# Two transformer layers on one core: how layer 0 keeps the exponentials of its eight chosen entries

## The chip, the cores and the metric

The kernel runs on one core of a Trainium2 chip. The metric is the device time of one execution in microseconds (us): the median of three runs, and beside it one execution taken by the hardware profiler, from which every duration of a single instruction comes. All data are fp32.

## The reference, cut to what matters

Two transformer layers work on 4 sequences of 512 tokens of width 512. Each layer adds an attention and a mixture of experts to its input. The change lies in the attention of layer 0, which has 16 heads of width 128. Each query of a head attends to two things: the keys of its own and the previous 128 tokens (the local part), and, among 128 entries that each compress 4 tokens, the 8 with the largest scores (the sparse part):

```python
sc = jnp.einsum('bhsd,bcd->bhsc', q, ck) * scale
sc = jnp.where(causal, sc, NEG)
tv, ti = jax.lax.top_k(sc, TOPK)                      # TOPK = 8
sel = (tv > NEG / 2).astype(sc.dtype)
m = jnp.max(tv, axis=-1, keepdims=True)
e = jnp.exp(tv - m) * sel
pw = e / jnp.maximum(e.sum(axis=-1, keepdims=True), 1e-09)
v_g = cv[jnp.arange(Bq)[:, None, None, None], ti]
ctx_sparse = jnp.einsum('bhsk,bhskd->bhsd', pw, v_g)
...
merged = (ctx_sparse + ctx_local) * 0.5
out = merged.transpose(0, 2, 1, 3).reshape(Bq, Sq, NH * D) @ Wo + bo
```

The kernel doesn't gather the chosen entries. It keeps a row of exponentials over all entries that a query may see, in which those that are not chosen are zero, and multiplies that row by all entries' values. So what is needed of each row of scores s is exp(s) where s is among the eight largest, and zero elsewhere.

## The kernel before

**Stages.** The start loads tables and normalises tokens. Layer 0's attention then runs in 32 steps: 8 groups of two heads, and for each group the 4 sequences (the loop of lines 1101 to 1160). After that comes layer 1 (from line 1171). In the profile, step 0 begins near 59 us and step 31 ends near 1440 us, so a step takes some 43 us.

**A step.** In each step i the heads 0 and 1 of the step are attended, while the projections of step i + 1 are made in between (`project`, lines 650 to 745: products p into the PSUM tag "mm" of three banks, line 675; their sums u, qb and lv on VectorE, lines 710 to 742; root mean squares by ScalarE's squares, line 575, and GpSimd's power, lines 577 and 578; ScalarE's scaling, line 689; turning by TensorE, lines 695 and 701, and ScalarE's copies, lines 696 and 702). For each head:

- `scores` makes the scores of 128 queries by four tiles of entries: TensorE writes sp (line 758), VectorE adds the causal mask (line 761), which gives s, 128 x 320. The 320 columns are the visible entries of the four tiles, 32, 64, 96 and 128 of them (`SEEN`, line 45). The local scores st go through ScalarE's exponential (line 771) and GpSimd's 0/1 mask (line 775).
- Then for each of the four tiles VectorE finds the eight largest of each row (line 779) and writes a copy rep of s in which these eight are replaced by NEG = -1e30 (line 780).
- Line 782 compares s with rep: 1 where they are equal, that is where an entry wasn't chosen. Line 783 adds NEG times that to s. Line 784 (ScalarE) takes the exponential of s, 320 elements, which is zero where NEG was added.
- `turn` transposes the result (TensorE, line 793) and copies it to SBUF (ScalarE, lines 794 and 795). `context` multiplies it by the entries' values (line 814) and the local exponentials by the local values (lines 809 and 811), divides by the sums and adds the two (lines 818 to 827).

After both heads, `output7` multiplies by the output weights (line 873) and adds to acc on VectorE (line 884).

**What sets the order.** A scheduler of the framework orders each engine's instructions, and an engine takes them strictly in that order. A few instructions are pinned to the order of the program. Into the steps other work is laid by a list of places (`run0`): in steps 0 to 2 the layernorms and the compressed entries (`compress`, lines 590 to 640: wd on VectorE at line 608, wB on TensorE at line 611, ck at line 628), in steps 3 and 4 the routing (lines 299 to 454, long chains of small VectorE instructions), in steps 5 to 22 the experts of layer 0 (lines 513 to 540: products hp_r at line 529, their rescue from PSUM by VectorE at line 532), and after that the combining of experts' results and the layernorms and weights' sums of layer 1 (lines 1016 to 1032 and 1207 to 1208).

**Buffers.** The pool wk0 has two buffers of the tag "s" (one 128 x 320 row tile each) and one of the tag "rep". The small table nws (line 194), used only at the start, is laid into the buffer of "rep". Tags are of fixed size, the largest of their users.

Of the kernel before, what the change touches and what calls it, by code (L numbers as in the profile page):

```python
# [12 lines left out]
F32 = mybir.dt.float32  # L13
I32 = mybir.dt.int32
AF = mybir.ActivationFunctionType
ALU = mybir.AluOpType
# [4 lines left out]
P = 128  # L21
# [3 lines left out]
TC = S // P  # L25
# [12 lines left out]
NEG = -1e30  # L38

SEEN = [slice(96, 128), slice(128, 192), slice(0, 96), slice(192, 320)]  # L40
LIMIT = 60.0
SCALE0 = 1.0 / math.sqrt(D)
# [7 lines left out]
def two_layers(ctx: ExitStack, tc: tile.TileContext, a: dict, out: bass.AP, large: bass.AP):  # L50
# [4 lines left out]
    V, G, A, PE = nc.vector, nc.gpsimd, nc.scalar, nc.tensor  # L55
# [11 lines left out]
    wk0 = layer0.enter_context(tc.tile_pool(name="att0", bufs=2))  # L67
    setup = ExitStack()

    sp0 = setup.enter_context(tc.tile_pool(name="setup", bufs=2, side="right"))  # L70


    def psum(tag, name):
        return ps.tile([P, 512], F32, tag=tag, name=name, bufs={"mm": 3, "sc": 3, "tr": 2}[tag])
# [70 lines left out]
    R = D // 2  # L145
# [45 lines left out]
    t2c = sp0.tile([P, 1, R], F32, tag="t2c", name="t2c", bufs=1)  # L191


    nws = wk0.tile([P, 2, R], F32, tag="rep", name="nws", bufs=1)
    own_ = lambda w, n, lo, m: nws[:, w, ds(lo, m)].unsqueeze(1).to_broadcast([P, n, m])

    def scale_weights():
# [551 lines left out]
    def scores(i, h, qkT):  # L749

        g, b = steps[i]
        nm = f"{g}_{b}_{h}"
        sp = psum("sc", f"sp_{nm}")
        seen = SEEN
        for t in range(TC):
            PE.matmul(sp[:, seen[t]], lhsT=qkT[:, h, ts(t, P)], rhs=ckT[:, b, 0 : 32 * (t + 1)],  # L758
                      start=True, stop=True)
        s = wk0.tile([P, SEEN[TC - 1].stop], F32, tag="s", name=f"s_{nm}")  # L760
        V.tensor_tensor(s, sp[:, 0 : SEEN[TC - 1].stop], cmask, ALU.add)
        lT = wk0.tile([P, TC * 2 * P - P], F32, tag="lT", name=f"lT_{nm}")
        for half in range(2):
            st = psum("sc", f"st{half}_{nm}")
            for t in (2 * half, 2 * half + 1):
                n = 256 if t + 1 < TC else 128
                PE.matmul(st[:, ds((t % 2) * 256, n)], lhsT=qkT[:, HG + h, ts(t, P)],  # L767
                          rhs=qkT[:, h, ds(t * P, n)], start=True, stop=True)
            for c in range(2):
                n = 256 if half + c < 2 else 128  # L770
                A.activation(lT[:, ds(half * 512 + c * 256, n)], st[:, ds(c * 256, n)], AF.Exp,  # L771
                             scale=norm_k[(i, h)][2 * half + c])
            n = 384 if half else 512
            dst = lT[:, ds(half * 512, n)]
            G.tensor_tensor(dst, dst, lmask.rearrange("p a w j -> p (a w j)")[:, 0:n], ALU.mult)  # L775
        top = small.tile([P, TC, 8], F32, tag="top", name=f"top_{nm}", bufs=2)
        rep = wk0.tile([P, SEEN[TC - 1].stop], F32, tag="rep", name=f"rep_{nm}", bufs=1)
        for t in range(TC):
            V.max(top[:, t, :], s[:, seen[t]])
            V.match_replace(rep[:, seen[t]], top[:, t, :], s[:, seen[t]], NEG)  # L780

        V.tensor_tensor(rep, s, rep, ALU.is_equal)
        V.scalar_tensor_tensor(s, rep, NEG, s, ALU.mult, ALU.add)
        A.activation(s, s, AF.Exp, scale=SCALE0)
        return s, lT

    def turn(i, h, em):
# [313 lines left out]
    for i, (g, b) in enumerate(steps):  # L1101
# [8 lines left out]
        cT = qp.tile([P, HG, S], F32, tag="cT", name=f"cT_{g}_{b}", bufs=1)  # L1110
        nc.sync.dma_start(out=cv0s[i % 2][96:P, 0:D], in_=cv[0:32, b, 0:D])
        em0, lT0 = scores(i, 0, now)
        turn_last(1)
        if more:
# [4 lines left out]
            if b == 2 and g + 1 in groups:  # L1119
                groups[g + 1][0][0] = load_block(g + 1, "wA")  # L1120
        run0((i, 0))
        em1, lT1 = scores(i, 1, now)
        sT0 = turn(i, 0, em0)
        run0((i, 1))
# [1151 lines left out]
```

## Time and profile before

| what | value |
|---|---|
| median of 3 runs | 2059.24 us (2058.99 to 2063.63) |
| the profiled execution | 2060.04 us, its span 2058.2 us |
| clock granted to TensorE | 0.995 |
| VectorE's row operations at lines 782 and 783, 64 each | 64.3 us and 42.9 us |
| ScalarE's exponential of s, line 784, 64 | 30.1 us |

TensorE is the engine "PE" of the profile (weight loads "PEld"), VectorE is "DVE", ScalarE "ACT", GpSimd "POOL". A line of the groups reads: line, engine, operation, output <- inputs with shapes, count | busy us, mean ns of one | idle time of the engine just before these instructions, and what ended it. A line of the timeline reads: start in us, duration in us, engine, line, operation, and in brackets the idle time before it and the instruction that ended that. A line of the windows reads: from:to, length, and each engine's busy us with its number of instructions.

### The profile page before, as it was taken

The page shows a single profiled execution, that of the slowest core. Times are in us where ns is not written, and L with a number is a line of the kernel's source. Part 1 is how long each engine was busy: PE and PEld are TensorE (multiplying, and loading weights), DVE is VectorE, ACT ScalarE, POOL GpSimd, SP SyncE. Part 2 cuts the span into 40 slices and gives each one's busy share as a digit, 9 for nine tenths or more (in the row PEclk, how much of TensorE's full clock was granted, in tenths as well). Part 3 has the DMA queues.
Part 4 walks back from the last instruction along what each step waited for, and adds up shares of the span by engine and source line. Part 5 has one row for each costly group of instructions (what it writes and reads, how often), then busy time and mean ns, then how long its engine had stood idle before and what let it go on. Part 6 is the DMA issues. An engine that isn't in the chain of part 4 may idle for free.

```text
span 2058.2 us, 28987 instructions
## 1 busy us (share of the span) xinstructions
PE 1982.5 (96%) x9514; PEld 1276.0 (62%) x9514; DVE 1545.9 (75%) x3799; ACT 864.3 (42%) x2600; POOL 745.4 (36%) x761
## 2 busy tenths in 40 slices
PE   7999999999999999999999998999999999999998
PEld 4666667777777777776667776776434445445442
DVE  7889987777776777786678888887696555557675
ACT  4544444444444444444444444454143432433332
POOL 4332235443332333334343444244114432422550
PEclk9999999999999999999999999999999999999999
DMA  7112133332433343244543222121317775773451
GB/s 251 58 42 62 32 123 114 134 131 93 136 118 119 114 144 116 93 136 174 189 161 116 73 88 67 48 73 62 120 32 264 258 257 204 261 245 117 151 160 58
DMA packets 98911, 267.29 MB, mean 130 GB/s; under 512 B 14400, under 2 KB 27840, under 8 KB 87488
## 3 DMA queue, kind: packets, MB, share of 16 engines
q0 software_dynamic: 27072, 148.91, 21.6%
q1 hardware_dynamic: 70528, 114.34, 16.6%
q10 hardware_dynamic: 1152, 2.10, 0.3%
q8 instruction: 78, 1.28, 0.3%
q14 instruction: 81, 0.66, 0.1%
HBM read 222.05 MB, written 42.73 MB: 129 GB/s over the span
## 4 chain that ended last, share of the span: by engine, by line
PE 73%; DVE 12%; ACT 4%; POOL 3%; issue 2%; DMA 1%; ACTq 0%; DVEq 0%; SPq 0%; POOLq 0%
PE p L675 21%; PE hp_r L529 12%; PE st L767 4%; PE ox L873 3%; PE st L1316 2%; PE oz L873 2%; PE qp L1292 2%; PE sp L758 2%; PE cx L1330 2%; DVE pS L1336 2%; PE ca L811 2%; PE o L1399 1%; PE trm_r L517 1%; ACT sq L575 1%; PE vp L1252 1%
## 5 line engine op out<-in xcount | busy, mean ns | idle before, releaser
L529 PE MATMUL hp_r<-we_r,xT_r 128*128 128x512 f32 (+1 forms) x592 | 224.7, 596 | 3.0 <-ACT xT_r L519 2.5
L481 POOL DMA_INDIRECT xr_r<-xnd,rows_r x72 | 87.5, 1216 | 348.1 <-PE trm_r L517 305.7
L775 POOL TENSOR_TENSOR lT<-lT,lmask 128x512 f32<-128x512 f32 (+1 forms) x128 | 152.1, 1196 | 150.7 <-ACT lT L771 150.6
L675 PE MATMUL p<-wT,x 128*128 128x384 f32 x512 | 179.8, 494 | 1.1 <-DVE wT L119 1.1
L675 PE MATMUL p<-wB,x 128*128 128x384 f32 x512 | 176.3, 488 | 3.0 <-DVE u L731 3.0
L675 PE MATMUL p<-wA,xnT 128*128 128x384 f32 x512 | 174.0, 490 | 0.1
L575 ACT ACTIVATE sq<-qb 128x128 f32<-128x128 f32 x384 | 118.9, 310 | 109.2 <-DVE qb L711 54.5
L1318 ACT ACTIVATE pT<-st 128x1024 f32<-128x1024 f32 x128 | 123.2, 1013 | 62.5 <-PE st L1316 56.8
L529 PEld LDWEIGHTS hp_r<-we_r,xT_r 128*128 128x128 f32 (+1 forms) x592 | 83.2, 170 | 99.0 <-issue 92.3
L675 PEld LDWEIGHTS p<-wB,x 128*128 128x128 f32 x512 | 93.9, 191 | 67.0 <-issue 9.9
L675 PEld LDWEIGHTS p<-wT,x 128*128 128x128 f32 x512 | 94.9, 194 | 63.4 <-issue 6.8
L675 PEld LDWEIGHTS p<-wA,xnT 128*128 128x128 f32 x512 | 95.1, 192 | 59.8 <-issue 1.9
L689 ACT ACTIVATE qb<-qb,ss 128x128 f32<-128x128 f32 x256 | 81.9, 390 | 107.3 <-POOL ss L578 103.8
L519 ACT COPY xT_r<-trm_r 128x512 f32<-128x512 f32 x72 | 41.8, 580 | 194.7 <-PE hp_r L529 181.9
L767 PE MATMUL st<-qkT 128*128 128x256 f32 (+1 forms) x512 | 116.0, 354 | 1.3 <-ACT qkT L702 1.3
L771 ACT ACTIVATE lT<-st,ss 128x256 f32<-128x256 f32 (+1 forms) x128 | 49.3, 444 | 158.2 <-PE st L767 158.1
L545 POOL DMA_INDIRECT row_r<-yd,slot_r x64 | 74.7, 1168 | 83.1 <-DVE row_r L1433 38.8
L767 PEld LDWEIGHTS st<-qkT 128*128 128x128 f32 x512 | 92.5, 191 | 12.0 <-ACT qkT L702 1.6
L578 POOL TENSOR_TENSOR ss<-ss,nhalf 128x6 f32<-128x6 f32 x64 | 94.3, 1474 | 5.3
L577 POOL TENSOR_SCALAR ss<-ss 128x6 f32<-128x6 f32 x64 | 31.1, 486 | 163.1 <-ACT sq L575 162.7
L675 PE MATMUL p<-wT,xnT 128*128 128x384 f32 x256 | 88.0, 487 | 0.0
L884 DVE TENSOR_TENSOR acc<-acc,ox 128x512 f32<-128x512 f32 (+1 forms) x96 | 82.3, 857 | 5.0 <-PE ox L873 4.4
(381 smaller groups left out, 4737.6 us busy)
## 6 DMA issues: line engine op xcount, KB each, us to landing
x<-xsd SPq DMA_DIRECT2D x112, 256.0 KB, 3.0
yd<-yr_r SPq DMA_DIRECT2D x72, 256.0 KB, 4.7
wA<-in_wA SPq DMA_DIRECT2D x16, 384.0 KB, 3.7
wB<-in_wB SPq DMA_DIRECT2D x16, 384.0 KB, 7.3
xnd<-xn SPq DMA_DIRECT2D x24, 256.0 KB, 2.0
accd<-acc SPq DMA_DIRECT2D x18, 256.0 KB, 2.0
acc<-in_x SPq DMA_DIRECT2D x16, 256.0 KB, 5.5
Wo<-in_Wo SPq DMA_DIRECT2D x8, 512.0 KB, 3.7
```

The costliest lines, as they stand in the source:

```text
L481: G.indirect_dma_start(out=out, out_offset=None, in_=src, in_offset=at_rows(idx))
L529: PE.matmul(hp[ts(h, m), :], lhsT=xT[:, k, ts(h, m)], rhs=w[:, ts(k, HID)], start=(k == 0), stop=(k == KC - 1))
L545: G.indirect_dma_start(out=x, out_offset=None, in_=self.yd, in_offset=at_rows(self.r.slot[:, k, n : n + 1]))
L575: A.activation(sq, x[:, h, :], AF.Square, accum_out=ss[:, h : h + 1])
L578: pin(G.tensor_tensor(ss, ss, nhalf[:, 0:n], ALU.pow))
L675: PE.matmul(p, lhsT=x[:, k, ts(c, P)], rhs=w[:, k, :], start=(k == 0), stop=(k == 1))
L689: A.activation(x[:, j, :], x[:, j, :], AF.Copy, scale=sq[t][:, j : j + 1])
L767: PE.matmul(st[:, ds((t % 2) * 256, n)], lhsT=qkT[:, HG + h, ts(t, P)], rhs=qkT[:, h, ds(t * P, n)], start=True, stop=True)
L775: G.tensor_tensor(dst, dst, lmask.rearrange("p a w j -> p (a w j)")[:, 0:n], ALU.mult)
L873: PE.matmul(p[:, ts(c, 256)], lhsT=left[:, ts(c, P)], rhs=right, start=new and c == 0, stop=True, skip_group_check=True)
L884: V.tensor_tensor(own, own, p, op)
L1318: A.activation(pt[:, ts(pair, 2), :], st, AF.Exp, scale=SCALE1)
```

## The change

The chosen entries are no longer marked. s and rep become the halves of one tile of 128 x 2 x 320, ScalarE takes the exponential of both at once, and VectorE subtracts the one from the other: where an entry wasn't chosen the two are the same number, and where it was chosen the second is exp(NEG) = 0. The buffer "rep" is gone, and nws gets a buffer of its own in the pool of the start.

```diff
-    nws = wk0.tile([P, 2, R], F32, tag="rep", name="nws", bufs=1)
+    nws = sp0.tile([P, 2, R], F32, tag="nws", name="nws", bufs=1)
...
-        s = wk0.tile([P, SEEN[TC - 1].stop], F32, tag="s", name=f"s_{nm}")
+        both = wk0.tile([P, 2, SEEN[TC - 1].stop], F32, tag="s", name=f"s_{nm}")
+        s, rep = both[:, 0, :], both[:, 1, :]
         V.tensor_tensor(s, sp[:, 0 : SEEN[TC - 1].stop], cmask, ALU.add)
...
         top = small.tile([P, TC, 8], F32, tag="top", name=f"top_{nm}", bufs=2)
-        rep = wk0.tile([P, SEEN[TC - 1].stop], F32, tag="rep", name=f"rep_{nm}", bufs=1)
         for t in range(TC):
             V.max(top[:, t, :], s[:, seen[t]])
             V.match_replace(rep[:, seen[t]], top[:, t, :], s[:, seen[t]], NEG)
 
-        V.tensor_tensor(rep, s, rep, ALU.is_equal)
-        V.scalar_tensor_tensor(s, rep, NEG, s, ALU.mult, ALU.add)
-        A.activation(s, s, AF.Exp, scale=SCALE0)
+        A.activation(both, both, AF.Exp, scale=SCALE0)
+        V.tensor_tensor(s, s, rep, ALU.subtract)
         return s, lT
```

`scores` is called 64 times, twice in each of the 32 steps. Nothing else is changed; since the scheduler orders the instructions anew, others may take another place in their queues.

## The prediction

> **What bounds the kernel now.** I read the page's busy times first, then its slices, the chain that ended last, the groups by form, a table of stretches, and last the timeline at the places where TensorE stops.
>
> ```profile
> PE 1982.5 (96%) x9514; PEld 1276.0 (62%) x9514; DVE 1545.9 (75%) x3799; ACT 864.3 (42%) x2600; POOL 745.4 (36%) x761
> ...
> PE   7999999999999999999999998999999999999998
> ...
> DVE  7889987777776777786678888887696555557675
> ...
> PE 73%; DVE 12%; ACT 4%; POOL 3%; issue 2%; DMA 1%; ACTq 0%; DVEq 0%; SPq 0%; POOLq 0%
> ```
>
> TensorE works 96% of the span. All that a change to VectorE can win is in the few per cent where TensorE waits. The stretches tell where these are (layer 0's attention is 59 to 1440):
>
> ```profile
> 59.00:170.00 111.00, 104.31 (x545) 74.77 (x544) 96.22 (x289) 56.86 (x185) 36.81 (x45) 1.00 0.14 48
> 170.00:700.00 530.00, 521.89 (x2531) 378.89 (x2530) 418.68 (x1169) 236.08 (x830) 191.28 (x180) 0.99 0.32 108
> 700.00:1000.00 300.00, 300.00 (x1459) 212.44 (x1458) 221.13 (x583) 133.67 (x469) 105.87 (x104) 1.00 0.41 140
> 1000.00:1250.00 250.00, 244.90 (x1232) 177.96 (x1231) 204.49 (x547) 115.56 (x414) 102.30 (x98) 1.00 0.34 112
> 1250.00:1440.00 190.00, 176.34 (x929) 132.44 (x927) 159.12 (x467) 88.33 (x310) 77.08 (x77) 1.00 0.19 62
> ```
>
> Length less the first busy time is TensorE's idle time: 6.7, 8.1, 0.0, 5.1 and 13.7 us, 33.6 together. From 700 to 1000, among the experts, there is none: nothing saved on VectorE is seen there. By the timeline nearly all of the 8.1 lies before 290, in steps 2 to 4. So only some 10 heads at the start and 16 at the end can show a gain; for the 38 in between (steps 5 to 23) the question is only whether something becomes late.
>
> The groups have the prices (busy us, mean ns):
>
> ```profile
> L782 DVE TENSOR_TENSOR rep<-s,rep 128x320 f32<-128x320 f32 x64 | 64.3, 1004 | 1.4
> L783 DVE SCALAR_TENSOR_TENSOR s<-rep,s 128x320 f32<-128x320 f32 x64 | 42.9, 670 | 1.4
> L761 DVE TENSOR_TENSOR s<-sp,cmask 128x320 f32<-128x320 f32 x64 | 31.0, 484 | 2.4 <-PE sp L758 2.2
> L784 ACT ACTIVATE s<-s 128x320 f32<-128x320 f32 x64 | 30.1, 470 | 56.5 <-DVE s L783 56.5
> ```
>
> Three VectorE operations have the same 320 elements, and two of them take far longer. The timeline shows why:
>
> ```profile
> 341.27 1.51 DVE L782 TENSOR_TENSOR rep<-s,rep 128x320 f32<-128x320 f32 x1
> 342.81 1.44 DVE L783 SCALAR_TENSOR_TENSOR s<-rep,s 128x320 f32<-128x320 f32 x1
> ```
>
> ```profile
> 341.17 1.26 POOL L954 TENSOR_TENSOR acc<-acc,bo 128x512 f32<-128x512 f32 x1
> 342.40 2.72 POOL L775 TENSOR_TENSOR lT<-lT,lmask 128x512 f32<-128x512 f32 x2
> ```
>
> While GpSimd runs an operation on tensors, the two-input VectorE operation beside it takes 1.4 to 1.5 us; elsewhere it takes 0.47 to 0.49. Line 761, which reads one input from PSUM, is never stretched.
>
> [...]
>
> **The change part by part.**
>
> *Removed:* lines 782 and 783, 64.3 + 42.9 = 107.2 us of VectorE, 1.67 a head.
>
> *Added on VectorE:* one subtraction of two SBUF inputs, 0.48 us where GpSimd is quiet. From above I bound it by line 782's mean, 1.00; it comes later than line 782 did, when GpSimd has often passed on, so I take 0.75, between 783's mean and 1.00. 64 x 0.75 = 48 us, so VectorE loses 59 us (bounds 43 to 76), 0.92 a head.
>
> *Exponential of 640 instead of 320:* the slope between line 784 (320, 470 ns) and line 1318 (1024, 1013 ns) is 0.77 ns an element, so 470 + 247 = 717[...]. 64 x 0.25 = 16 us more on ScalarE, which is 42% busy. Bounds: 0.63 (line 536, 512 elements) and 1.01 (line 1318).
>
> *A new wait:* the exponential starts right after the last line 780 instead of after 783, and VectorE's subtraction waits for it. By the order of the built kernel, in steps 5 to 22 for head 1 nothing stands between line 780 and the subtraction, for head 0 one projection sum; in steps 24 to 28 two. Without cover VectorE's stretch is, from the end of 780, 0.05 (pass to ScalarE, as 344.25 to 344.29 for line 784) + 0.72 + 0.05 + 0.48 to 1.0 = 1.3 to 1.8 us, against 1.67 before: about even. Queued behind the subtraction are line 532 (rescue of hp_r) or 710 and 717 (rescue of p), so TensorE's three "mm" banks. On ScalarE the exponential of head 1 now stands ahead of head 0's copies, lines 794 and 795. At the place shown above ScalarE is busy with lines 689 and 771 from 341.2 to 343.1, so the exponential ends near 343.9 and the subtraction at 344.4 to 345.3, where 783 ended at 344.25: 0.2 to 1.0 later. It is covered:
>
> ```profile
> 344.18 0.68 DVE L532 TENSOR_TENSOR yr_r<-hp_r,we_r 128x512 f32<-128x512 f32 x1
> 344.79 0.56 DVE L717 TENSOR_TENSOR u<-p,u 128x384 f32<-128x384 f32 x1
> 346.08 0.56 DVE L718 TENSOR_TENSOR u<-p,u 128x384 f32<-128x384 f32 x1 [0.73 <-PE p L675]
> 347.64 0.16 DVE L818 TENSOR_SCALAR sums<-ca 128x3 f32<-128x3 f32 x1 [1.00 <-PE ca L811]
> ```
>
> VectorE itself waits 0.73 and 1.00 us for TensorE right after, TensorE next writes the bank that line 532 frees at 348.8, and reads head 0's sT at 347.9, which is copied by 344.5. I take nothing; if the cover is gone it is 20 x 0.6 = 12 us.
>
> *Buffers:* nws elsewhere, one tile for two. No instruction of its own, and both halves of a tile have the life that s and rep had. Nothing.
>
> *Where TensorE waits (gain each, from the timeline):* first 59 to 290.
>
> ```profile
> 163.22 1.12 DVE L782 TENSOR_TENSOR rep<-s,rep 128x320 f32<-128x320 f32 x1
> 164.26 0.54 DVE L717 TENSOR_TENSOR u<-p,u 128x384 f32<-128x384 f32 x1
> 164.73 0.15 DVE L604 RECIPROCAL wsm<-wsm 128x1 f32<-128x1 f32 x1
> 164.80 1.21 DVE L783 SCALAR_TENSOR_TENSOR s<-rep,s 128x320 f32<-128x320 f32 x1
> ...
> 166.53 0.92 DVE L608 TENSOR_SCALAR wd<-ident,w 128x128 f32<-128x128 f32 x4
> ```
>
> TensorE stands 1.24 us for wd, which was behind both removed operations; in the built order it comes ahead of the subtraction: 1.3. At 145.7 it waits 1.18 for ck, whose GpSimd step waited behind line 666 (1.27 us), now earlier: 0.7. At 94 to 96 VectorE is late in step 0: 0.4. At 189.7 line 895 holds TensorE 1.90 us; VectorE has no gap from 160.6 on, but the steps before also lost their wait: 0.35. At 210 and at 227 to 236 (routing's small instructions) 0.4 each, at 268 to 277 0.3; at 251 nothing, since there the subtraction comes ahead. Sum 3.85.
>
> The end, 1000 to 1440: the stall of 1.8 us that recurs in steps 24 to 28 goes through qb, squares (line 575), GpSimd's ss (578), ScalarE's 689, the context and line 731; no removed operation is in it, so it stays. Near 1146 and 1225 0.3, at 1308 (783 in the chain) 0.4, at 1265 nothing (the sum L711 now comes after the subtraction, but GpSimd's 577 and 578 go ahead of a 775). At 1430 VectorE's line 1208 stands 1.19 us for the store of acc, behind GpSimd's 1022, which ran behind the two 775 and now runs ahead of them: 1.3. Sum 2.0.
>
> Given back: in steps 0 to 2 the longer exponential stands ahead of lines 689 and 702 in ScalarE's queue, 3 x 0.25, and 0.25 at 251: 1.0. Net 3.85 + 2.0 - 1.0 = 4.85. The profiled execution took 2060.04 (its span 2058.2, 1.8 lie around it), 0.8 above the median of the runs shown. 2060.04 - 4.85 = 2055.2, as a median 2054.4.
>
> **The rivals.**
>
> *All hidden.* For it: TensorE idle 0.0 from 700 to 1000 and the recurring stall of steps 24 to 28 without removed work. Against: the wait at 167. It keeps the 1.3 of that place less the 1.0 given back, so 2059.
>
> *The lead carries.* At the start and the end VectorE is at 84 to 87%; if half of what each of these 26 heads saves reaches TensorE, 26 x 0.92 / 2 = 12 us: 2047. For it: no gap on VectorE from 160.6 to 189. Against: most stalls name ScalarE or GpSimd.
>
> *Slower.* VectorE stands for the exponential in the 20 heads without cover, and the rescue of hp_r and p behind it frees the "mm" banks too late. Price 20 x 0.6 = 12, less the gains 5.85: 2066. It decides from the point where line 532 ends after TensorE's next write to its bank, 3.9 us later than now at the place shown. That slack speaks against it.
>
> *Not what it says:* were the subtraction stretched to 1.5 us each time and the exponential at 1.0, VectorE would still save 0.1 a head; it falls into the first rival.
>
> **How the numbers follow.** The forecast 0.45 (2051 to 2057), all hidden 0.25 (2057 to 2060.5), the lead carries 0.20 (2044 to 2051), slower 0.10 (2061 to 2070). The range 2048.5 to 2060.5 leaves out the slower case and about half of the lead. 0.3%, about what a measurement of this kernel can tell from no change, is 6.2 us: faster is below 2053.1, the lead and half of the forecast, 0.42; slower above 2065.4, most of the slower case, 0.08; the rest, 0.50, within.
>
> **What would show it.** The subtraction's mean 0.5 to 1.0 us, the exponential's 0.70 to 0.75, VectorE's busy time 1470 to 1503. From 700 to 1000 TensorE still without idle time (idle there: the slower rival). No wait for wd near 167, and 1250 to 1440 at 12 us idle instead of 13.7. The forecast is wrong if the new wait shows as idle time of TensorE behind line 532, 710 or 717, or if the scheduler's other order opens a stall at a place that I took as untouched.

## The result and the profile after

| | before | after |
|---|---|---|
| median, 20 runs each | 2062.97 us (2058.99 to 2067.69) | 2056.53 us (2053.93 to 2060.88) |
| profiled execution, span | 2058.2 us | 2056.0 us |

The ratio is 0.9973, with a 95% interval of 0.9965 to 0.9981: 5.6 us of 2063, where 4.85 were forecast. The median of the kernel before rose from 2059.2 to 2063.0 when its three runs became twenty; the ratio, not the difference of any two medians, says what the change did. It is a gain clear of no change, though smaller than the 0.3% that the prediction took as the line between faster and the same.

The executions also differ in their mean granted clock (1 is full speed), and the time goes with it. Of 96 executions of the kernel before, taken beside the experiments below, the 23 with a clock of 0.993 took 2063.8 us on average and the 18 with 0.996 took 2060.4. The 20 of the changed kernel had 0.9949 on average, those 96 had 0.9942. If each of the 20 is set against the mean of the executions before that had its own clock, the change is worth 4.8 us. Whether the other 0.8 us are chance, or came with the waits that are gone, no run shows.

The page after: busy times, the slices, and the shares of the chain that ended last.

```profile
PE 1985.9 (97%) x9514; PEld 1275.7 (62%) x9514; DVE 1482.4 (72%) x3735; ACT 877.3 (43%) x2600; POOL 743.1 (36%) x761
...
PE   7899999999999999999999999999999999999998
...
DVE  7878976776766667676668888887696655557775
...
PE 71%; DVE 11%; ACT 4%; POOL 3%; issue 2%; DMA 1%; SPq 0%; DVEq 0%; ACTq 0%; POOLq 0%
```

VectorE lost 63.5 us of work (1545.9 to 1482.4) and the kernel less than a tenth of that. The groups of the operations that took the place of the old ones (busy us, mean ns, idle time before and its releaser):

```profile
L782 ACT ACTIVATE s<-s 128x640 f32<-128x640 f32 x64 | 47.0, 735 | 16.9 <-DVE s L780 16.8
L783 DVE TENSOR_TENSOR s<-s 128x320 f32<-128x320 f32 x64 | 39.4, 615 | 51.2 <-ACT s L782 51.2
```

VectorE's 107.2 us became 39.4. But it now stands 51.2 us in front of the subtraction, waiting for ScalarE: the new wait is no small one. The stretches show what TensorE made of it (length, then TensorE's busy time):

```profile
59.00:170.00 111.00, 103.55 (x530) 73.77 (x529) 88.34 (x282) 57.76 (x185) 35.90 (x45) 0.98 0.13 46
170.00:700.00 530.00, 522.63 (x2543) 379.05 (x2542) 392.62 (x1139) 240.16 (x830) 188.97 (x179) 0.99 0.31 107
700.00:1000.00 300.00, 300.00 (x1458) 211.72 (x1456) 205.50 (x576) 136.19 (x469) 106.59 (x102) 1.00 0.40 140
1000.00:1250.00 250.00, 244.70 (x1231) 177.63 (x1231) 195.56 (x536) 117.25 (x410) 102.77 (x98) 1.00 0.34 113
1250.00:1440.00 190.00, 177.88 (x940) 134.31 (x939) 155.41 (x462) 92.40 (x317) 77.09 (x78) 1.00 0.19 62
```

From 700 to 1000 TensorE still has no idle time; from 1250 to 1440 it is 12.1 us instead of 13.7, as forecast. From 59 to 170 it is 7.45, more than the 6.7 of before: something was lost there.

**One thing has to be taken out before the two profiles are compared.** The granted clock of TensorE (the third number from the end) dips for short stretches, and differently in each execution. Three stretches, of before and then of after:

```profile
20.00:40.00 20.00, 14.78 (x53) 9.17 (x50) 18.31 (x51) 8.33 (x29) 10.04 (x16) 0.83 0.78 272
60.00:80.00 20.00, 18.25 (x99) 12.85 (x97) 18.95 (x68) 11.12 (x33) 7.25 (x10) 1.00 0.08 28
250.00:280.00 30.00, 25.91 (x141) 18.85 (x142) 26.06 (x80) 13.48 (x53) 7.54 (x7) 0.94 0.21 66
```

```profile
20.00:40.00 20.00, 15.50 (x48) 9.71 (x49) 17.37 (x50) 7.68 (x27) 9.62 (x15) 0.74 0.74 265
60.00:80.00 20.00, 15.91 (x82) 11.47 (x81) 16.38 (x58) 9.93 (x26) 6.38 (x9) 0.91 0.08 28
250.00:280.00 30.00, 27.11 (x150) 19.08 (x149) 25.09 (x75) 13.48 (x55) 8.13 (x8) 0.89 0.21 68
```

Length times (1 - clock), summed, is 3.4 + 0 + 1.8 = 5.2 us before and 5.2 + 1.8 + 3.3 = 10.3 after; over all stretches of 20 us from 0 to 2040 it is 8.8 and 13.8. A dip is a piece of 3.41 us at half the clock, or two or three such pieces in a row (6.83 and 10.24 us). By length and clock I estimate that a piece costs at most half its length, 1.7 us (less where it falls on idle time); in the profile after, four products of line 675 took 2.77 us in the piece at 70.81, and eight took 2.75 behind it, from 76.39. One of before and one of after:

```profile
254.00:257.41 3.41, 2.97 (x16) 2.59 (x17) 2.19 (x15) 1.84 (x5) 0.00 (x0) 0.50 0.00 0
```

```profile
70.81:74.22 3.41, 3.41 (x8) 1.80 (x7) 1.78 (x4) 0.00 (x0) 0.00 (x0) 0.50 0.22 82
```

Up to the start of layer 1 the profile before lost 6.8 us to such pieces and the one after 10.2. So two single spans can't be compared as they are, and a step is judged by more than one profile below.

### The profile page after: what moved, and what is told of

Read it like the earlier page. It is cut to its first block, busy times and chain, and to the rows that moved or that the text cites. A ratio compares the mean times of both kernels' runs of the same rounds, so it can differ in the third digit from the quotient of the medians.

```text
span 2056.0 us, 28900 instructions
## 1 busy us (share of the span) xinstructions
PE 1985.9 (97%) x9514; PEld 1275.7 (62%) x9514; DVE 1482.4 (72%) x3735; ACT 877.3 (43%) x2600; POOL 743.1 (36%) x761
## 4 chain that ended last, share of the span: by engine, by line
PE 71%; DVE 11%; ACT 4%; POOL 3%; issue 2%; DMA 1%; SPq 0%; DVEq 0%; ACTq 0%; POOLq 0%
PE p L675 21%; PE hp_r L529 12%; PE st L768 4%; PE ox L872 3%; PE st L1315 3%; PE oz L872 2%; PE qp L1291 2%; PE sp L758 2%; PE cx L1329 2%; DVE pS L1335 2%; PE ca L810 2%; PE o L1398 1%; PE trm_r L517 1%; PE vp L1251 1%; ACT sq L575 1%
## 5 line engine op out<-in xcount | busy, mean ns | idle before, releaser
L768 PEld LDWEIGHTS st<-qkT 128*128 128x128 f32 x512 | 92.3, 190 | 12.1 <-ACT qkT L702 1.6
```

## The experiments

Each ratio below is the time against that of the kernel before, measured beside the experiment, with its 95% interval; "at the same clock" means the comparison made above for the change. The edits are shown against the changed kernel. To place a gain I took from each trace the start of the reciprocal of the sums (line 821 of before, one per head) and subtracted that of before. A row tells how many us the head 0 of a step comes later (+) or earlier (-) than in the profile before. "Layer 1" is the same for the first product of layer 1 (line 1238 of before), "span" the difference of the spans, and "clock" what the pieces of slow clock up to layer 1 cost at most, less the 6.8 us of before.

| kernel | 0 | 1 | 2 | 3 | 4 | 5 | 6 | 22 | 27 | 30 | 31 | layer 1 | span | clock |
|---|---|---|---|---|---|---|---|---|---|---|---|---|---|---|
| after | 4.1 | 3.4 | 1.4 | 1.4 | 3.0 | 1.6 | 1.23 | 1.23 | 0.4 | 1.3 | -1.4 | 0.2 | -2.2 | 3.4 |
| buffers alone | 0.8 | 0.8 | 0.8 | 0.2 | 0.7 | 0.7 | 0.67 | 0.67 | 2.1 | 2.3 | 2.3 | 4.0 | 3.9 | 3.4 |
| steps 5 to 23 | -0.4 | -0.4 | -0.4 | -1.1 | -0.8 | -0.8 | -1.24 | -1.24 | -0.7 | -0.7 | -1.1 | 1.7 | 1.3 | 1.7 |
| steps 0 to 4, 24 to 31 | 1.6 | 1.2 | -0.8 | -0.9 | -2.3 | -3.6 | -3.60 | -3.60 | -4.2 | -3.6 | -6.3 | -5.0 | -7.9 | -1.7 |
| all but step 0 | -0.3 | -0.6 | -2.5 | -2.8 | -4.2 | -5.6 | -5.98 | -5.97 | -6.6 | -5.8 | -8.5 | -7.2 | -8.0 | -3.4 |
| one operation given back | 3.1 | 3.4 | 1.2 | 2.7 | 2.6 | 2.6 | 2.22 | 2.22 | 3.5 | 4.6 | 3.8 | 6.5 | 6.8 | 6.8 |
| step 31 alone | 0.5 | 0.5 | 0.5 | -0.2 | 0.2 | 0.2 | 0.18 | 0.19 | 0.5 | 0.7 | -1.7 | -0.4 | -0.3 | -1.7 |
| all but 0 and 30 | -0.2 | -0.5 | -2.4 | -2.8 | -4.2 | -5.5 | -5.88 | -5.87 | -6.5 | -6.4 | -9.1 | -7.8 | -8.5 | -3.4 |

Four things are read at once. From step 6 to step 22 every row stands still to a hundredth: TensorE runs those steps through with either form. The second row, whose instructions are in the order of before on every engine, still wanders by some 4 us, and that is nearly all the clock: 4.0 us late at layer 1, with 3.4 us more of slow clock. The rows of steps 5 to 23 and of the operation given back, which win nothing by their ratios either, are likewise late by what the clock cost. Then, every row with the new form in step 31 gains at its head 0 and gives 1.3 to 1.6 us of it back before layer 1 begins (without the row of the operation given back, which meets slow clock there). And in layer 1, where the order of instructions is the same in all these kernels, rows still move by up to 3 us: that is scatter. Ratios decide whether there is a gain, and this table only where.

**The buffers alone.** s and rep share a tile and nws has its own; the operations are the old ones.

```diff
-        A.activation(both, both, AF.Exp, scale=SCALE0)
-        V.tensor_tensor(s, s, rep, ALU.subtract)
+        V.tensor_tensor(rep, s, rep, ALU.is_equal)
+        V.scalar_tensor_tensor(s, rep, NEG, s, ALU.mult, ALU.add)
+        A.activation(s, s, AF.Exp, scale=SCALE0)
```

> The buffers alone: s and rep as halves of one tile, nws in its own buffer, but the old comparison, the old addition and the exponential over 320. The order of all engines' instructions is that of the kernel before. My theory (the gain comes from VectorE's shorter work and the order it leads to): 0 us, ratio 0.999 to 1.001. Rival (the buffers win the time): ratio near 0.997, the whole gain.

Measured: 1.0001 (0.9992 to 1.0011). The buffers cost and win nothing.

**The new form in some steps only.** The two forms of the last edit stand in a condition on the step, here for the middle:

```diff
+        if 5 <= i < 24:
             A.activation(both, both, AF.Exp, scale=SCALE0)
             V.tensor_tensor(s, s, rep, ALU.subtract)
+        else:
...
```

> The new form only in steps 5 to 23, the old one in steps 0 to 4 and 24 to 31. My theory: VectorE sheds some 35 us, the time stays within 0.5 us of the kernel before, ratio 0.9995 to 1.0005, since TensorE has no idle time there. Rival (VectorE's time counts wherever it is spent): 38 of 64 heads, so 0.6 of the gain, ratio 0.9984. Rival (the new wait costs where no work covers it): slower, ratio above 1.001.

Measured: 1.0001 (0.9993 to 1.0009). In 38 of 64 heads VectorE's saving is worth nothing that can be measured, and the new wait costs nothing either. How it is covered, at the place that the prediction looked at (VectorE, the profile after, which there is 1.23 us later than before):

```profile
342.19 0.28 DVE L780 MATCH_REPLACE8 s<-top,s 128x128 f32<-128x128 f32 x1
344.99 1.20 DVE L783 TENSOR_TENSOR s<-s 128x320 f32<-128x320 f32 x1 [2.53 <-ACT s L782]
346.11 0.68 DVE L532 TENSOR_TENSOR yr_r<-hp_r,we_r 128x512 f32<-128x512 f32 x1
346.71 0.54 DVE L717 TENSOR_TENSOR u<-p,u 128x384 f32<-128x384 f32 x1
347.36 0.56 DVE L718 TENSOR_TENSOR u<-p,u 128x384 f32<-128x384 f32 x1
348.86 0.16 DVE L817 TENSOR_SCALAR sums<-ca 128x3 f32<-128x3 f32 x1 [0.95 <-PE ca L810]
```

and what ScalarE did meanwhile:

```profile
342.44 1.28 ACT L689 ACTIVATE qb<-qb,ss 128x128 f32<-128x128 f32 x4 [1.23 <-POOL ss L578]
343.63 0.70 ACT L772 ACTIVATE lT<-st,ss_k 128x256 f32<-128x256 f32 x2
344.23 0.72 ACT L782 ACTIVATE s<-s 128x640 f32<-128x640 f32 x1
```

VectorE stands 2.53 us, 1.76 of it because the exponential waits for lines 689 and 772 ahead of it in ScalarE's queue (342.47 to 344.23). The subtraction ends at 346.19, that is 344.96 in the time of before, where line 783 had ended at 344.25: 0.7 later. VectorE's next wait of before, 0.73 for TensorE's p at line 718, is gone: the delay went into it. The one after it, at line 817, is nearly what it was (0.95, before 1.00). So the new wait is paid by the work that VectorE no longer has and by a wait that it had anyway.

> The new form only in steps 0 to 4 and 24 to 31, the old one in steps 5 to 23. My theory: the whole gain of the change, ratio 0.9965 to 0.998. Rival (VectorE's time counts everywhere): 0.4 of it, ratio 0.9989.

Measured: 0.9973 (0.9962 to 0.9984), the ratio of the whole change. As far as the intervals tell, all of the gain lies in 26 heads.

**The old form in step 0.** The table shows the changed kernel 4.1 us late at its first head. Part of that is the clock: the kernel with the new form in steps 0 to 4 and 24 to 31, without a dip from 60 to 80, is 1.6 late. But in both the new wait wasn't covered, and TensorE stood the same 2.49 us. VectorE in the profile after:

```profile
63.04 0.15 DVE L601 TENSOR_REDUCE wmx<-w 128x1 f32<-128x4 f32 x1
64.91 0.79 DVE L783 TENSOR_TENSOR s<-s 128x320 f32<-128x320 f32 x1 [1.72 <-ACT s L782]
...
67.25 2.70 DVE L608 TENSOR_SCALAR wd<-ident,w 128x128 f32<-128x128 f32 x4
```

and TensorE:

```profile
66.91 0.60 PE L253 MATMUL trx<-ident,xn 128*128 128x128 f32 x4
70.00 1.31 PE L611 MATMUL wB<-wd,ones_sq 128*128 128x512 f32 x2 [2.49 <-DVE wd L608]
```

VectorE stood 1.72 us for the exponential. The four operations of wd, 0.93 us at 66.25 before, came a microsecond later and took 2.70. Before, only the last of the four was left when GpSimd's mask began at 66.81, and none was stretched; now the mask ran from 67.31 to 69.60, and the second and third took 1.35 and 1.09 us instead of 0.33. The second ends 0.15 us behind the mask's first operation (67.31 to 68.65), the third 0.15 behind its second (68.62 to 69.60): stretched beside GpSimd as line 782 was.

```diff
+        if i > 0:
             A.activation(both, both, AF.Exp, scale=SCALE0)
             V.tensor_tensor(s, s, rep, ALU.subtract)
+        else:
...
```

> The new form in steps 1 to 31, the old one in step 0. In the profile of the changed kernel VectorE stands 1.7 us for the exponential in step 0, the diagonal wd (line 608) comes later and TensorE waits 2.5 us for it, where it didn't before. My theory: this wait goes, so 2 to 3 us faster than the changed kernel, ratio to the kernel before 0.9955 to 0.9968. Rival (the wait only takes up slack that another wait uses next): as the changed kernel, 0.997 to 0.9975.

Measured: 0.9959 (0.9946 to 0.9972), median 2053.27 us. TensorE's wait in step 0 is gone (wB starts at 66.97, right behind p). Beside 0.9973 that is 2.9 us; the intervals overlap a little. There were only five executions, at a high clock (0.9960 on average); at the same clock the difference to the changed kernel is 1.9 us.

**One VectorE operation given back.**

```diff
         V.tensor_tensor(s, s, rep, ALU.subtract)
+        V.tensor_tensor(rep, s, rep, ALU.min)
```

> The changed kernel with one more VectorE operation of 128 x 320 a head (the lesser of s and rep into rep, which nobody reads), so VectorE does two such operations a head again, as before the change; ScalarE's exponential stays right after line 780. If VectorE's shorter time is what wins at the two ends: most of the gain goes, ratio to the kernel before 0.9985 to 1.001. If it is the order alone (wd, line 1208 and the store of acc come ahead, which this leaves): the gain stays, 0.997 to 0.998.

Measured: 1.0001 (0.9992 to 1.0011). The whole gain goes, although GpSimd's addition at line 1022 keeps its new place in step 31 and VectorE no longer waits for the store behind it: TensorE still stands 2.41 us for the context near 1437. So the new place of that addition doesn't bring the gain by itself, and VectorE's time counts. A second reading stays: the scheduler moved other instructions as well, and this run doesn't part the operation's own time from these moves.

**Three other ways to the same rows.** The exponential of s early, beside the search, and only that of rep behind it; the exponential before the search; the subtraction on GpSimd. In the first two edits the added exponential stands right after the mask (line 761 of before), in the first one into a tile em of its own:

```diff
+        A.activation(em, s, AF.Exp, scale=SCALE0)
...
-        A.activation(both, both, AF.Exp, scale=SCALE0)
-        V.tensor_tensor(s, s, rep, ALU.subtract)
+        A.activation(rep, rep, AF.Exp, scale=SCALE0)
+        V.tensor_tensor(em, em, rep, ALU.subtract)
```

> The exponential of s goes right after the mask into a tile of its own, while VectorE searches the eight largest; after line 780 only the exponential of rep is left (320 elements, 0.47 us instead of 0.735). If the new wait behind line 780 costs: 1 to 2 us faster than the changed kernel, ratio 0.9963 to 0.997. If ScalarE's queue costs (64 instructions more of 0.2 us overhead, ahead of lines 689 and 771): slower than it, 0.9975 to 0.999.

Measured: 0.9990 (0.9982 to 0.9998), 1.7 thousandths slower than the change. By its trace the start is about as good as the others' (-3.2 us at step 6), and then it loses 4.4 us between steps 23 and 27 and more until 29; near 1185 and 1226 TensorE waits 1.1 us each time for line 689, which the changed kernel doesn't have. 64 more instructions in ScalarE's queue fit that, each of some 0.2 us beside its elements by my estimate (the means of 470 ns for 320 elements before and 735 for 640 after leave 205 for none). But the edit changes buffers too (s has one instead of two), and the order changed widely; no run parts these.

```diff
+        A.activation(s, s, AF.Exp, scale=SCALE0)
...
-            V.match_replace(rep[:, seen[t]], top[:, t, :], s[:, seen[t]], NEG)
+            V.match_replace(rep[:, seen[t]], top[:, t, :], s[:, seen[t]], 0.0)
...
-        A.activation(both, both, AF.Exp, scale=SCALE0)
```

> The exponential (320 elements, once) comes before the search: VectorE finds the eight largest exponentials and replaces them by zero in the copy, then subtracts. Nothing follows line 780 but the subtraction, so the wait at the end is gone; a wait for the exponential stands ahead of the search instead. [...] If a wait costs less where other VectorE work can go ahead of it: ratio 0.9955 to 0.997. If it costs the same anywhere: 0.997 to 0.998.

Measured: 0.9970 (0.9961 to 0.9980), as the change. Moving the wait ahead of the search is worth nothing that can be measured.

```diff
-        V.tensor_tensor(s, s, rep, ALU.subtract)
+        G.tensor_tensor(s, s, rep, ALU.subtract)
```

> The subtraction on GpSimd instead of VectorE: VectorE sheds another 39 us and never waits for the exponential; GpSimd gets 64 operations of some 1 us in its queue, among lines 577 and 578, which the projections wait for. If GpSimd's queue counts at the ends: slower than the changed kernel, ratio 0.998 to 1.001. If VectorE's time is all that counts: faster, 0.995 to 0.9965.

Measured: 0.9985 (0.9977 to 0.9993). From 59 to 2040 VectorE is busy 27.5 us less than in the changed kernel (1406.4, after 1433.9) and GpSimd 53.8 us more (771.3, after 717.4), 0.84 a subtraction, and nearly half of the gain is lost (the intervals overlap a little). By its trace TensorE waits 1.5 us for the subtraction on GpSimd; the rest of the loss was not placed.

**Step 31 alone.** The condition is i == 31.

> The new form only in the last step, 31; the old one in steps 0 to 30. In the order of GpSimd this moves one thing: the addition of wo_b (line 1022 of before) goes ahead of the two lines 775 of head 1. My theory: the store of acc starts some 3.7 us earlier, VectorE's line 1208 no longer waits for it, and TensorE's wait of 3.0 us near 1430 falls to about 1.2, so 1.5 to 2.7 us, ratio 0.9987 to 0.9993. Rival (the gain there needs the VectorE time saved in the steps before): under 0.7 us, 0.9997 or more.

Measured: 0.9990 (0.9983 to 0.9998); at the same clock that is 0.8 us. Its trace gains 2.4 us from step 30 to 31 (0.7 to -1.7), much as the others with the new form there. The timeline of GpSimd, first before, then this kernel (its line 1026 is 1022 of before, its 776 is 775):

```profile
1424.49 3.24 POOL L775 TENSOR_TENSOR lT<-lT,lmask 128x512 f32<-128x512 f32 x2 [1.95 <-ACT lT L771]
1427.69 1.27 POOL L1022 TENSOR_TENSOR acc<-acc,wo_b 128x512 f32<-128x512 f32 x1
```

```profile
1423.58 1.45 POOL L1026 TENSOR_TENSOR acc<-acc,wo_b 128x512 f32<-128x512 f32 x1 [0.73 <-DVE xn L247]
1425.00 2.23 POOL L776 TENSOR_TENSOR lT<-lT,lmask 128x512 f32<-128x512 f32 x2
```

VectorE's wait for the store of acc is gone, and TensorE's for the context, again before and this kernel:

```profile
1433.09 0.46 PE L811 MATMUL ca<-lv,lT 128*128 128x129 f32 x2 [3.02 <-DVE ctx L827]
```

```profile
1431.52 0.46 PE L815 MATMUL ca<-lv,lT 128*128 128x129 f32 x2 [1.18 <-DVE ctx L831]
```

But it doesn't keep all of that. Five microseconds later TensorE waits for a copy of ScalarE (line 835 of before), which now stands behind the four activations of line 825 of the next head; before and this kernel:

```profile
1436.90 1.13 PE L873 MATMUL ox<-Wo,cT 128*128 128x256 f32 x4 [0.24 <-ACT cT L835]
```

```profile
1436.42 1.13 PE L877 MATMUL ox<-Wo,cT 128*128 128x256 f32 x4 [1.33 <-ACT cT L839]
```

When layer 1 begins, 1.0 us is left of the 2.4 (0.69 at step 30, -0.36 there). Two heads of 64, in whose step GpSimd runs one addition sooner, so bring some 1 us by the trace and 0.8 to 2 by the ratio.

**The old form in steps 0 and 30.** In step 30 the changed kernel lost 0.8 us.

> The new form in all steps but 0 and 30, where the old one stays. In step 30 the changed kernel lost 0.8 us: ScalarE's exponential of 640 elements stands ahead of the squares (line 575) of the next step's projection, whose root mean square TensorE waits for. My theory: that comes back, 0.5 to 1.0 us faster than the kernel with the old form in step 0 alone (ratio 0.9959 there), so 0.9952 to 0.9957. Rival (step 31 hides it anyway, since its stalls wait for other work): the same as that one, 0.9957 to 0.9962.

Measured: 0.9951 (0.9936 to 0.9965), median 2051.74 us, the fastest of all, from five executions; the interval covers the ratio of the kernel with the old form in step 0 alone, so only the traces tell the two apart. The 0.8 us of step 30 come back (-6.5 at 27, -6.4 at 30), but not for the reason that I had written down. In the kernel with the old form in step 0 alone, GpSimd has

```profile
1380.39 0.55 POOL L236 TENSOR_TENSOR mv<-mv,nhalf 128x1 f32<-128x1 f32 x1 [0.67 <-DVE mv L235]
1381.02 0.41 POOL L577 TENSOR_SCALAR ss<-ss 128x6 f32<-128x6 f32 x1
```

and in this one

```profile
1380.27 0.56 POOL L577 TENSOR_SCALAR ss<-ss 128x6 f32<-128x6 f32 x1 [0.63 <-ACT sq L575]
```

with the layernorm's line 236 behind it: ss comes 0.6 us sooner, then qb, which TensorE waits for. The last of ScalarE's squares ends at 1380.03 there and at 1380.18 here, so they were not late: it was GpSimd's order, not ScalarE's longer exponential.

## Why the prediction was right, point by point

- **Where it can count.** Only TensorE's waits at the two ends were to be won. Shown: the middle alone 1.0001, the ends alone 0.9973, and rows that stand still from step 6 to 22.
- **The prices.** The subtraction was put at 0.75 us (bounds 0.48 to 1.00) and took 0.615; the exponential at 0.72 and took 0.735; VectorE was to lose 59 us (43 to 76) and lost 63.5. One reading was too coarse: that an operation beside GpSimd "takes 1.4 to 1.5 us" holds for 19 of line 782's 64. But all 50 that took over 0.55 us end 0.35 or 0.36 us behind the GpSimd instruction that was under way when they began, and so do all 24 such subtractions of after: what it cost these is the rest of that instruction. Four more of line 782 began with over 0.5 us of a GpSimd instruction left and took 0.47 to 0.49 all the same (two beside line 545, one beside 578, and one beside the mask of line 775, at 1424.90). And "never stretched" rests on little: all 64 of line 761 took 0.47 to 0.49, 10 of them with over 0.5 us of a GpSimd instruction left, but only one of these beside a mask (62.98).
- **The uncovered wait in steps 5 to 22.** Put at nothing: right. It was to end 0.2 to 1.0 us later than line 783 had, and ended 0.7 later. What I called "about even", 1.3 to 1.8 us without cover, leaves out ScalarE's queue: in one head of each of these 18 steps VectorE stands 2.5 us, 45 of the 51.2.
- **The first 290 us.** 3.85 less 1.0 were to be won. At step 6 the kernel with the new form at both ends stands at -3.6 and the changed kernel at 1.2, with 1.7 us less and 3.4 us more of slow clock than before: some 2 us won in either. Here the sum came within a microsecond and its terms didn't. The loss in step 0 was put at a quarter of a microsecond (the longer exponential ahead of lines 689 and 702); TensorE waited 2.5 us, because I priced what stands behind the exponential on ScalarE and not what stands behind the subtraction on VectorE, which is wd. The wait for wd near 167 was to vanish, 1.3; it fell from 1.24 to 0.84, since wd now waits for ScalarE's line 603, which stands behind 689. The ck near 146 went from 1.18 to 0.18, as written. The waits at 189 and 210 to 236 stayed (the first of them is 1.90 us before and 1.91 in the kernel with the old form in step 0 alone). Near 268 to 274, where I had put 0.3, TensorE's two waits of 0.82 and 0.43 us are gone in that kernel, and its row gains 1.3 from step 4 to 5.
- **The end.** 2.0 were to be won. From step 22 to layer 1 the changed kernel wins 1.0 (1.2 to 0.2) and the one with the new form at both ends 1.4, with no slow clock in these stretches in any of the three profiles: half of the forecast or a little more. The store of acc, 1.3, gave 1.85 on TensorE's wait itself (3.02 to 1.17) and 2.4 to 2.7 at the head 0 of step 31, but 1.0 to 1.4 were left at layer 1, chiefly because of the wait for ScalarE's copy, which I had left out. The recurring stall of steps 24 to 28 stayed. Near 1265 I had put nothing and it won 0.9; in step 30 I had priced no change, and a third line 236 ahead of 577 cost 0.8.
- **The rivals.** "All hidden" falls with the ratio's interval. "The lead carries" at 12 us falls too, though VectorE's time is the source. "Slower" had the right mechanism at the wrong place: a wait for the exponential with work that TensorE needs behind it did cost, in step 0, and only there.

So the places and the prices were right, and that the total came so near is partly luck: the misses, 2 to 2.5 us lost in step 0, 0.8 in step 30 and 1.3 behind step 31 against gains near 268, 1265 and 1430, go both ways and nearly cancel. The places found in the profiles add up to some 3 us, where the ratio says 5.6 and the comparison at the same clock 4.8; what makes up the rest stays open.

## What to carry to other kernels

Ask first in which stretches the busiest engine waits; here a saving elsewhere was worth nothing, and a new wait there cost nothing. A wait that a change adds is priced by what stands behind it on the engine that waits, step by step, the first one and the last one too, since the steps are not alike. Where a scheduler orders the queues, part of a gain can come from one instruction that moved on a third engine: compare the orders, and try the change in one step alone. Follow a gain to the end of its stage before counting it (2.4 us at the last step were 1.0 when the next layer began), and lay the clock of each profile beside the difference of the two.

## What was not expected of the hardware

The clock granted to TensorE does not dip just anywhere. In the profiles before and after every dip is made of the pieces of 3.41 us at 0.50 shown above, but for the one that runs past the end of each span (from 2056.24 and 2053.95). Each of the nine others begins while TensorE stands in a wait of 1.90 us or more, or up to 1.01 us behind its end: 254.00 in the wait of 2.46 us that ends at 254.44, 70.81 behind the one of 2.49 that ends at 70.00. Not every such wait has one: before, the 2.84 us near 1267 and the 3.02 near 1433 have none, and of the wait at line 1452 of before, near 2002, the 2.05 us of before have none, while the 2.07 of after have one, at 2002.75. So which dips an execution meets differs, and between these two profiles that is the 5.0 us from 8.8 to 13.8 above. Whether a change that shortens such a wait wins part of a dip besides, no run here tests.

And a VectorE operation with one tensor input (wd, line 608) was stretched beside GpSimd like those with two: 28 of the 32 in the two profiles took 0.32 to 0.36 us, and the other four 0.97 to 1.45, among them the 1.35 and 1.09 of step 0, each ending 0.14 or 0.15 us behind an operation of GpSimd's mask.
